# Moving attention's constants and the projections of sequence 0 into the LoRA stage before it, and the output bias from POOL to VectorE

## The chip, the cores and the metric

The kernel runs on one core of a Trainium2 chip. The metric is the device time in microseconds from launch to end; lower is better. Engines are named as in the profile: PE is TensorE (PEld its weight loads), DVE is VectorE, ACT is ScalarE, POOL is GpSimd and SP is SyncE, which issues the DMAs here.

## The reference

The program is a macaron block of six stages over 16 sequences of 512 tokens with 256 features. Each stage normalizes its input without learned scale and adds its result to `x`:

```
x = x + 0.5 * ffn(layernorm(x))       # 4-bit quantised feed-forward
x = x + mamba(layernorm(x))           # selective scan
x = x + 0.5 * ffn(layernorm(x))
x = x + 0.5 * lora(layernorm(x))      # base weights + 8 gated experts of rank 8
x = x + attention(layernorm(x))       # the stage that the change is about
x = x + 0.5 * lora(layernorm(x))
```

The two stages that matter compute, for one sequence:

```
lora:      result = x @ base_w.T + base_b
           gating = softmax(x @ router_w.T + router_b)      # in bf16
           mid    = x @ lora_A
           out    = result + 2 * einsum(mid, lora_B, gating)

attention: q, k, v = x @ Wq + bq, x @ Wk + bk, x @ Wv + bv  # 16 heads of 16
           scores  = q k^T / 4 + alibi, causal mask
           out     = softmax(scores) v  @ Wo + bo
```

## The kernel before

**Where the data lie.** From the third stage on, all 16 sequences stay in SBUF as tiles `x0` to `x15`, 128 partitions by 4 blocks of 128 tokens by 256 features, in float32. Attention and the LoRA stages read and write them in place.

**How the order comes about.** The kernel is written for a framework that gives each tile its place in memory, adds the waits between engines, and orders the instructions of each engine ahead of time by its own estimate of when they can run. An instruction can so be placed far ahead of where the text of the kernel has it, as far as free buffers allow. Attention's matmuls and transposes (`matmul`, `transpose`, lines 1175 to 1179) are kept in the order of the text; LoRA's are not. Tile pools that are opened one after the other share memory: a tile of a later pool waits for the last reader of the earlier tile in its place. In the kernel before, the pools of attention are opened when those of LoRA are closed.

**A LoRA stage** (`lora_phase`, lines 946 to 1060) runs as a pipeline over the sequences: in round `b`, `norm(b)` makes the normalized `xh`, `turn(b - 1)` transposes it into `xT`, `base(b - 2)` multiplies by base weights, router and `lora_A` at once (`ob`, line 998), adds to `x` and makes the softmax of the gates (lines 1002 to 1023), and `experts(b - 3)` transposes the gated rows (`ct`, line 1033), multiplies by `lora_B` (`o`, line 1042) and adds to `x` (line 1047). It runs twice, before attention and after it.

**Attention** (`attn_phase`) begins with constants: the four weights and five bias tiles by DMA (lines 1084 to 1098; `bob` is the output bias, spread over all partitions), row numbers, slopes, eight tiles each for `q` and `k` with the extra rows that carry ALiBi and the row maximum (lines 1132 and 1137), two masks, two tiles `mx` and three `va`. Then it projects sequence 0, all of it, ahead of its main loop.

`project(b)` is a generator that hands back control between pieces. The first piece is the LayerNorm on DVE (statistics, lines 1189 and 1190; `v`, line 1196; a logarithm and an exponential on ACT, lines 1198 and 1199, as a first guess of the inverse root; two Newton steps, lines 1201 to 1205; `xh`, line 1210) and, at its end, the output bias, added to `x` in advance by POOL (line 1214). Then come the transposes (line 1225 empties them), the products for q and k, whose rows SP copies head by head into the tiles of the ring (8 DMAs for each of 4 products, line 1249), and the values with their bias (`va`, line 1266).

The main loop goes over units of four heads, four units to a sequence, six steps to a unit. A step computes scores of unit `u` to find row maxima (`peak_score`; DVE adds the mask, line 1299, and takes the maximum, line 1303) and, interleaved, the scores of unit `u - 1` once more with the maximum subtracted (`weigh_score`), whose exponential ACT takes (`eT`, line 1349). Unit `u - 2` is multiplied with the values (`apply`), divided (`divide`) and, at the end of a sequence, multiplied by `Wo` and added to `x` (`close`, line 1407). Between the steps `aside` puts in pieces of the next sequence's `project` and of the last ones' `divide` and `close`, by costs written at each `yield`.

In the text of the kernel each product or transpose is one call; in the trace a float32 matmul or a transposed block shows as one or several records.

Of the kernel before, what the change touches and what calls it, by code (L numbers as in the profile page):

```python
# [8 lines left out]
F32 = mybir.dt.float32  # L9
# [26 lines left out]
def macaron_kernel(  # L36
# [909 lines left out]
    def lora_phase(weights, last):  # L946
        wx, lb, br = weights
        W = D + NE + NR
        with tc.tile_pool(name="l", bufs=2) as lp, tc.tile_pool(
# [101 lines left out]
            for b in range(NB + 3):  # L1051
                if 0 <= b - 3:
                    experts(b - 3)
                if 0 <= b - 2 < NB:
                    base(b - 2)
                if 0 <= b - 1 < NB:
                    turn(b - 1)
                if b < NB:
                    norm(b)
        return copies[-1]  # L1060


    def attn_phase(behind):
# [15 lines left out]
        with tc.tile_pool(name="aw", bufs=1) as aw, tc.tile_pool(  # L1079
            name="a", bufs=2  # L1080
        ) as ap, tc.tile_pool(name="a_s", bufs=1, space=PSUM) as ps_s, tc.tile_pool(
            name="a_ps", bufs=2, space=PSUM
        ) as ps:
            wp = {}
# [8 lines left out]

            bq_t = aw.tile([P, KD], F32, name="bq_t")
# [33 lines left out]
            qs, ks = [], []  # L1128
# [12 lines left out]
            qms = {}  # L1141

            def at(b, j):
                return (b % 2) * NJ + j
# [19 lines left out]
            mxs, vas = [], []  # L1164
            for r in range(3):
                if r < 2:
                    mx = aw.tile([P, NC4, 4, 32], F32, name=f"mx{r}")
                    nc.gpsimd.memset(mx, 0.0)
                    mxs.append(mx)
                va = aw.tile([P, NC4, VW], F32, name=f"va{r}")  # L1170
                nc.gpsimd.memset(va, 1.0)
                vas.append(va)


            def matmul(out, **kw):
                tc.keep_in_program_order(nc.tensor.matmul(out, **kw))  # L1176

            def transpose(out, in_):
                tc.keep_in_program_order(nc.tensor.transpose(out, in_, ident))  # L1179

            def project(b):

                x = xs[b]
                st = ap.tile([P, NC4, 6], F32, name="st", tag="st")
                mv = ap.tile([P, NC4, 2], F32, name="mv", tag="mv")
                for c in range(NC4):
                    nc.vector.bn_stats(out=st[:, c, :], in_=x[:, c, :])
                    nc.vector.bn_aggr(out=mv[:, c, :], in_=st[:, c, :])  # L1190


                v = ap.tile([P, NC4], F32, name="v", tag="v")
                g = ap.tile([P, NC4], F32, name="g", tag="g")
                rs = ap.tile([P, NC4], F32, name="rs", tag="rs")
                nc.vector.tensor_scalar(v, mv[:, :, 1], EPS, None, op0=ALU.add)  # L1196
                with tc.issue_after(loaded.ins):
                    nc.scalar.activation(rs, v, AF.Ln)
                nc.scalar.activation(rs, rs, AF.Exp, scale=-0.5)
                for _ in range(2):  # L1200
                    nc.vector.tensor_tensor(g, rs, v, op=ALU.mult)
                    nc.vector.scalar_tensor_tensor(
                        g, g, -0.5, rs, op0=ALU.mult, op1=ALU.mult
                    )
                    nc.vector.scalar_tensor_tensor(
                        rs, g, 1.5, rs, op0=ALU.add, op1=ALU.mult
                    )
                xh = ap.tile([P, NC4, D], F32, name="xh", tag="xh", bufs=1)
                for c in range(NC4):
                    nc.vector.tensor_scalar(  # L1210
                        xh[:, c, :], x[:, c, :], mv[:, c, 0:1], rs[:, c : c + 1],
                        op0=ALU.subtract, op1=ALU.mult,
                    )
                nc.gpsimd.tensor_tensor(  # L1214
                    xs[b], xs[b], bob.unsqueeze(1).to_broadcast([P, NC4, D]), op=ALU.add
                )
                yield 0, False
                xT = ap.tile([P, KD, SEQ], F32, name="xT", tag="xT", bufs=1)
                for k in range(KD):
                    p = ps.tile([P, SEQ], F32, name="p", tag="mm")  # L1220
                    for c in range(NC4):
                        transpose(
                            p[:, c * P : (c + 1) * P], xh[:, c, k * P : (k + 1) * P]
                        )
                    nc.scalar.copy(xT[:, k, :], p)
                    yield 2, False
                for m in range(KD):
                    for name, ring in (("q", qs), ("k", ks)):
                        p = ps.tile([P, SEQ], F32, name="p", tag="mm")
                        for k in range(KD):  # L1230
                            matmul(
                                p, lhsT=wp[name][:, k, m * P : (m + 1) * P],
                                rhs=xT[:, k, :], start=(k == 0), stop=(k == KD - 1),
                            )
                            if k == 0:
                                yield 3, True
                        r = ap.tile([P, SEQ], F32, name=f"{name}u", tag=f"{name}u")
                        if name == "q":
                            nc.scalar.activation(
                                r, p, AF.Identity, bias=bq_t[:, m : m + 1], scale=0.25  # L1240
                            )
                        else:
                            nc.vector.tensor_scalar(
                                r, p, bk_t[:, m : m + 1], None, op0=ALU.add
                            )

                        for h in range(8):
                            i, j = h % 4, 2 * m + h // 4
                            nc.sync.dma_start(
                                out=ring[at(b, j)][32 * i : 32 * i + HD, :],  # L1250
                                in_=r[HD * h : HD * (h + 1), :],
                            )
                        yield 3, False
                for half in range(2):
                    p = ps.tile([P, 2, D], F32, name="p", tag="mm")
                    for c in range(2):
                        t = 2 * half + c
                        for k in range(KD):
                            matmul(
                                p[:, c, :], lhsT=xT[:, k, t * P : (t + 1) * P],  # L1260
                                rhs=wp["v"][:, k, :], start=(k == 0), stop=(k == KD - 1),
                            )
                        if c == 0:
                            yield 3, True
                    dst = vas[b % 3][:, 2 * half : 2 * half + 2, : NH * HV]
                    nc.vector.tensor_tensor(
                        dst.rearrange("p c (h e) -> p c h e", e=HV)[:, :, :, :HD],
                        p.rearrange("p c (h e) -> p c h e", e=HD),
                        bvb.rearrange("p (h e) -> p h e", e=HD).unsqueeze(1).to_broadcast(
                            [P, 2, NH, HD]  # L1270
                        ),
                        op=ALU.add,
                    )
                    yield 3, False


            def peak_score(b, j, part, pair, s):

                q, k = qs[at(b, j)], ks[at(b, j)]
                for n, (t, off) in enumerate(PEAK[part]):  # L1280
                    ln = (t + 1) * P
                    for i in range(2):
                        r0 = 32 * (2 * pair + i)
                        matmul(
                            s[:, i, off : off + ln],
                            lhsT=q[r0 : r0 + 32, t * P : (t + 1) * P],
                            rhs=k[r0 : r0 + 32, :ln],
                            start=(n == 0), stop=(n == len(PEAK[part]) - 1),
                            skip_group_check=True,
                        )  # L1290
                        yield

            def peak_max(b, j, part, pair, s):
                mx = mxs[(b * NJ + j) % 2]
                t, off = PEAK[part][0]
                w = len(PEAK[part]) * P

                own = s[:, :, off + t * P : off + t * P + w]
# [86 lines left out]
            def close(b, os):  # L1385
# [9 lines left out]
                for half in range(2):  # L1395
                    r = ps.tile([P, 2, D], F32, name="r", tag="mm")
                    for c in range(2):
# [6 lines left out]
                        if c == 0:  # L1404
                            yield 3, True
# [198 lines left out]
```

## Time and profile before

| What | Value |
|---|---|
| Time, median of three runs | 4422.94 us (4412.12 to 4426.61) |
| Profiled execution, its own time | 4425.58 us |
| Span of the profiled execution, first to last instruction | 4423.8 us |
| Mean granted TensorE clock | 0.960 |
| Start of the first LoRA stage (first load of its weights) | 2992.45 us |
| End of its last matmul | 3132.0 us |
| First score of attention | 3161.84 us |
| Start of the second LoRA stage (its first memset) | 4280.81 us |

Times of single instructions and windows below are microseconds from the start of this span. An answer of the timeline has start, length, engine, line, operation, output and inputs, shapes and count; a bracket at its end has the engine's idle time before it and what ended that. A window has its bounds and length, the busy time of PE, PEld, DVE, ACT and POOL with the number of instructions in brackets, the granted clock of TensorE (1.00 is full), the share of the DMA engines and GB/s. A row of the waits reads: engine, tile and line, what it waited for, microseconds in all, times, the longest.

### The profile page before, as it was taken

What the parts mean: (1) busy time and instruction counts of PE and PEld (TensorE: products, weight loads), DVE (VectorE), ACT (ScalarE), POOL (GpSimd) and SP (SyncE); (2) the same over time, 40 slices, a digit from 0 to 9 for tenths busy, and PEclk for the clock granted to TensorE, in tenths of its full rate; (3) what the DMA queues carried; (4) which work ended last, traced back from release to release, by engine and by line L of the source; (5) the groups of instructions that cost most, each with busy time, mean ns of one, the idle gap of its engine ahead of it and who ended that gap; (6) DMA issues with size and microseconds to landing.
All of it is one profiled execution on the core that took longest, in us unless ns stands there. A gap on an engine that the chain in (4) does not pass through costs nothing. (4 is left out here: it accounts for less than half of the span.)

```text
span 4423.8 us, 51434 instructions
## 1 busy us (share of the span) xinstructions
PE 4037.3 (91%) x18786; PEld 2208.9 (50%) x18786; DVE 3744.2 (85%) x4919; ACT 2333.3 (53%) x3485; POOL 1680.5 (38%) x965
## 2 busy tenths in 40 slices
PE   7999978888888898988887999998899999999988
PEld 4666633333333333333333666766455555555546
DVE  9999839999999999999999899987677777777755
ACT  4444346777777777777664444436233334344345
POOL 3000038888888888888888000000100000000000
PEclk9999989999999999999999999999799999999979
DMA  4000033444444444444441200000100000000002
GB/s 147 15 20 15 15 132 126 135 136 137 132 137 136 135 139 137 126 135 133 133 137 39 103 1 1 1 1 4 32 11 18 18 16 18 15 18 18 13 8 69
DMA packets 120895, 305.16 MB, mean 69 GB/s; under 512 B 25329, under 2 KB 45362, under 8 KB 104002
## 3 DMA queue, kind: packets, MB, share of 16 engines
q1 hardware_dynamic: 120642, 301.88, 21.7%
q8 instruction: 148, 2.42, 0.2%
q14 instruction: 105, 0.86, 0.1%
HBM read 239.68 MB, written 45.35 MB: 64 GB/s over the span
## 5 line engine op out<-in xcount | busy, mean ns | idle before, releaser
L486 POOL TENSOR_TENSOR bx<-dtu,bc 128x1024 f32<-128x1024 f32 x512 | 1193.6, 2358 | 47.5 <-DVE h L882 47.4
L492 PE MATMUL y<-g,ident 128*128 128x512 f32 x2048 | 1007.3, 630 | 130.1 <-DVE g L489 129.8
L882 DVE TENSOR_TENSOR_SCAN h<-da,bx 128x1024 f32<-128x1024 f32 x384 | 879.7, 2291 | 85.5 <-ACT da L483 48.6
L483 ACT ACTIVATE da<-dt,a_neg 128x511 f32<-128x511 f32 x1024 | 702.9, 688 | 217.7 <-DVE hs L882 117.6
L492 PEld LDWEIGHTS y<-g,ident 128*128 128x128 f32 x2048 | 389.0, 199 | 709.3 <-issue 461.2
L1349 ACT ACTIVATE eT<-s 128x768 f32<-128x768 f32 (+1 forms) x384 | 338.2, 881 | 495.1 <-PE s L1176 495.1
L1176 PE MATMUL s<-k,q 32*128 32x256 f32 (+3 forms) x2048 | 500.3, 498 | 1.2 <-DMA k<-ku 1.2
L489 DVE TENSOR_TENSOR g<-h,bc 128x1024 f32<-128x1024 f32 x384 | 468.8, 1221 | 28.6 <-DVE h L882 1.4
L1176 PE MATMUL s<-qm,k 32*128 32x512 f32 (+3 forms) x2048 | 409.5, 497 | 37.3 <-ACT eT L1349 37.2
L1299 DVE TENSOR_TENSOR s<-s,mask 128x256 f32<-128x256 f32 (+1 forms) x384 | 199.8, 520 | 263.1 <-PE s L1176 256.8
L1303 DVE TENSOR_REDUCE mx<-s 128x2 f32<-128x1024 f32 (+3 forms) x512 | 409.7, 821 | 12.2
L1214 POOL TENSOR_TENSOR x<-x,bob 128x1024 f32<-128x1024 f32 x16 | 37.5, 2342 | 880.4 <-DVE xh L1210 878.0
L486 POOL TENSOR_TENSOR g<-hs,bc 128x1024 f32<-128x1024 f32 x128 | 301.2, 2353 | 157.7 <-DVE hs L882 140.5
L290 ACT ACTIVATE sl<-g 128x352 f32<-128x352 f32 x256 | 118.0, 464 | 385.2 <-PE g L285 380.4
L1176 PEld LDWEIGHTS s<-k,q 32*128 32x128 f32 x2048 | 232.1, 199 | 172.7 <-issue 95.3
L957 POOL MEMSET cb<- 128x4 f32 x6 | 0.3, 105 | 779.4 <-PE o L330 561.3
L882 DVE TENSOR_TENSOR_SCAN hs<-da,bx 128x1024 f32<-128x1024 f32 x128 | 292.0, 2281 | 2.5 <-ACT da L483 2.5
L492 PE MATMUL p<-xT,w_in 128*128 128x512 f32 x500 | 242.3, 608 | 19.7 <-ACT xT L483 10.0
L1176 PEld LDWEIGHTS s<-qm,k 32*128 32x128 f32 x2048 | 181.9, 198 | 86.0 <-ACT eT L1349 80.3
L483 ACT ACT_TABLE_LOAD x170 | 218.1, 1283 | 3.0
L515 POOL MEMSET xs<- 128x12 f32 x2 | 0.2, 110 | 513.9 <-DMA xd<-x 513.9
L285 PE MATMUL g<-wgT,xT 128*128 128x352 f32 x512 | 182.6, 467 | 0.0
(240 smaller groups left out, 6950.0 us busy)
## 6 DMA issues: line engine op xcount, KB each, us to landing
bc<-bd SPq DMA_DIRECT2D x128, 1024.0 KB, 6.5
xs<-xc SPq DMA_DIRECT2D x240, 256.0 KB, 4.7
xc<-xp SPq DMA_DIRECT2D x60, 256.0 KB, 2.0
x<-_attn_hidden_states_dram SPq DMA_DIRECT2D x16, 512.0 KB, 7.2
xd<-x SPq DMA_DIRECT2D x16, 512.0 KB, 2.6
xo<-xd SPq DMA_DIRECT2D x16, 512.0 KB, 3.5
xe<-xo SPq DMA_DIRECT2D x16, 512.0 KB, 2.6
x<-xe SPq DMA_DIRECT2D x16, 512.0 KB, 10.2
```

Of the source, the lines that this page charges most:

```text
L285: nc.tensor.matmul(dst, lhsT=xT[:, k, c * P : (c + 1) * P], rhs=w[:, k, f0 : f0 + HF], start=(k == 0), stop=(k == KD - 1),)
L290: nc.scalar.activation(sl, g, AF.Silu)
L483: return tc.keep_in_program_order(nc.scalar.activation(out, in_, func, **kw))
L486: tc.keep_in_program_order(nc.gpsimd.tensor_tensor(out, in0, in1, op=op))
L489: tc.keep_in_program_order(nc.vector.tensor_tensor(out, in0, in1, op=op))
L492: tc.keep_in_program_order(nc.tensor.matmul(out, **kw))
L882: tc.keep_in_program_order(nc.vector.tensor_tensor_scan(flat(h), flat(das[t % 2]), flat(bxs.pop(t)), 0.0, op0=ALU.mult, op1=ALU.add,))
L1176: tc.keep_in_program_order(nc.tensor.matmul(out, **kw))
L1214: nc.gpsimd.tensor_tensor(xs[b], xs[b], bob.unsqueeze(1).to_broadcast([P, NC4, D]), op=ALU.add)
L1299: nc.vector.tensor_tensor(own, own, mask[:, :w].unsqueeze(1).to_broadcast([P, 2, w]), op=ALU.add)
L1303: nc.vector.tensor_reduce(mx[:, t, 2 * pair : 2 * pair + 2, RM], s[:, :, off : off + (t + 1) * P], axis=AX.X, op=ALU.max,)
L1349: nc.scalar.activation(eT[:, 2 * pair : 2 * pair + 2, e0 : e0 + w], s[:, :, :w], AF.Exp)
```

## The change

The constants of attention become a generator, `constants`, with pauses; the first LoRA stage draws from it in rounds 1 to 15, one piece a round and two in odd rounds, the rest in round 15. Their pool `aw` is opened ahead of LoRA's pools. Sequence 0, whose LoRA result is complete after round 15, is normalized in round 16 by LoRA's own `norm` (square root and reciprocal), transposed in round 17 by LoRA's `turn`, and projected by `heads`, the second half of the old `project`, which now takes its transposed input, its pools and its matmul as arguments: the first q and k products in round 17, the others and the values in round 18. Attention's own pools are opened after that, where LoRA's were. The second LoRA stage has neither argument and is as before. For every sequence the POOL add of `bob` goes, and DVE adds it in two halves after the values. The rest of the diff is indentation and names.

```diff
-    def lora_phase(weights, last):
+    def lora_phase(weights, last, beside=None, heads=None):
 ...
                 if b < NB:
                     norm(b)
+                if heads is not None:
+                    if 0 < b < NB:
+                        next(beside, None)
+                        if b % 2:
+                            next(beside, None)
+                    if b == NB - 1:
+                        for _ in beside:
+                            pass
+                    if b == NB:
+                        norm(0)
+                    if b == NB + 1:
+                        turn(0)
+                        first = heads(0, xTs.pop(0), lp, ps, "tr", nc.tensor.matmul)
+                        for _ in range(4):
+                            next(first)
+                    if b == NB + 2:
+                        for _ in first:
+                            pass
 ...
-    def attn_phase(behind):
+    def attn_phase(weights):
 ...
+        def constants(aw):
             # weights, bvb, bob by DMA
+            yield
             # bq_t, bk_t, prow, is_s, neg_m, slope, pos
+            yield
             for i in range(2):
                 for j in range(NJ):
                     # one q and one k tile
+                    yield
             # id16, mask, mask_k
+            yield
             # mx, va
 ...
         def project(b):
 ...
-                nc.gpsimd.tensor_tensor(
-                    xs[b], xs[b], bob.unsqueeze(1).to_broadcast([P, NC4, D]), op=ALU.add
-                )
                 yield 0, False
                 # transposes into xT
+            yield from heads(b, xT, ap, ps, "mm", matmul)
+
+        def heads(b, xT, ap, ps, tag, matmul):
             # q and k products with their DMAs
             for half in range(2):
                 # values with bvb into va
+                xc = x[:, 2 * half : 2 * half + 2, :]
+                nc.vector.tensor_tensor(
+                    xc, xc, bob.unsqueeze(1).to_broadcast([P, 2, D]), op=ALU.add
+                )
                 yield 3, False
 ...
+        with tc.tile_pool(name="aw", bufs=1) as aw:
+            behind = lora_phase(weights, False, constants(aw), heads)
+            # attention's pools, table load after behind, main loop
-            for _ in project(0):
-                pass
 ...
-    behind = lora_phase(weights, False)
-    attn_phase(behind)
+    attn_phase(weights)
     lora_phase(weights, True)
```

## The prediction

> **What bounds the kernel now.** I read the page first, then the chain of waits and the waits at the seam between the first LoRA stage and attention, then the timeline of two attention sequences, then windows cut at what those showed.
>
> ```profile
> span 4423.8 us, 51434 instructions
> ...
> PE 4037.3 (91%) x18786; PEld 2208.9 (50%) x18786; DVE 3744.2 (85%) x4919; ACT 2333.3 (53%) x3485; POOL 1680.5 (38%) x965
> ...
> L1214 POOL TENSOR_TENSOR x<-x,bob 128x1024 f32<-128x1024 f32 x16 | 37.5, 2342 | 880.4 <-DVE xh L1210 878.0
> ```
>
> TensorE carries the time. POOL's bias add seems cheap: 37.5 us in all on an engine that is free in attention. What it costs others is not in that row. The waits around the seam:
>
> ```profile
> POOL prow L1101 <- PE o L1042: 139.5, 1, 139.5
> ...
> SPq L1087 <- PE o L1042: 136.7, 1, 136.7
> ```
>
> All of attention's constants wait for the last LoRA matmul. The windows of the seam (busy time of each engine, then granted clock, DMA share, GB/s):
>
> ```profile
> 3132.03:3145.22 13.19, 0.00 (x1) 0.04 (x1) 12.49 (x53) 0.00 (x0) 5.90 (x11) 0.50 0.33 100
> 3145.22:3161.84 16.62, 14.65 (x41) 7.63 (x41) 12.77 (x41) 3.03 (x8) 4.69 (x2) 0.84 0.09 20
> 3161.84:3191.13 29.29, 28.13 (x71) 10.74 (x70) 18.31 (x40) 3.08 (x6) 2.35 (x1) 0.60 0.20 44
> ```
>
> TensorE is idle for 13.19 us while VectorE makes constants, then projects sequence 0 for 16.62 us; the first score is at 3161.84. Third, the timeline at one POOL add, and at a later one (start, length, engine, line):
>
> ```profile
> 3929.34 2.34 POOL L1214 TENSOR_TENSOR x<-x,bob 128x1024 f32<-128x1024 f32 x1 [65.93 <-DVE xh L1210]
> 3929.71 2.00 DVE L1196 TENSOR_SCALAR v<-mv 128x4 f32<-128x4 f32 x1
> ...
> 3931.74 0.20 ACT L1198 ACTIVATE rs<-v 128x4 f32<-128x4 f32 x1 [3.48 <-DVE v L1196]
> ...
> 3932.09 0.79 ACT L1349 ACTIVATE eT<-s 128x768 f32<-128x768 f32 x1
> ...
> 3932.93 1.00 PE L1176 MATMUL s<-qm,k 32*128 32x384 f32 x1 [2.29 <-ACT eT L1349]
> ```
> ```profile
> 3997.41 0.81 ACT L1349 ACTIVATE eT<-s 128x768 f32<-128x768 f32 x1 [0.88 <-PE s L1176]
> ...
> 3997.61 2.35 POOL L1214 TENSOR_TENSOR x<-x,bob 128x1024 f32<-128x1024 f32 x1 [65.93 <-DVE xh L1210]
> ...
> 3998.27 0.58 PE L1176 MATMUL s<-qm,k 32*128 32x384 f32 x1
> ```
>
> A VectorE instruction of 4 elements takes 2.00 us beside the add; where it meets no POOL work the same line takes 0.17. ScalarE's logarithm waits for it, the exponential of the scores is queued behind that logarithm, and TensorE waits 2.29 us for the exponential. At 3997 no later sequence is left to normalize, so `v` isn't there, and nothing waits. The windows from add to add show the price:
>
> ```profile
> 3929.34:3932.20 2.86, 1.30 (x4) 0.29 (x2) 2.33 (x5) 0.43 (x3) 2.34 (x1) 1.00 0.00 0
> 3932.20:3939.02 6.82, 6.09 (x33) 3.72 (x34) 4.39 (x12) 2.19 (x4) 0.00 (x0) 0.50 0.16 34
> 3939.02:3997.61 58.59, 58.26 (x493) 31.54 (x492) 44.00 (x74) 24.54 (x32) 0.00 (x1) 1.00 0.07 16
> 3997.61:4060.34 62.73, 62.40 (x529) 34.02 (x528) 47.48 (x79) 26.78 (x35) 2.36 (x2) 1.00 0.08 18
> ```
>
> A sequence with the wait takes 68.27 us (the first three rows), one without it 62.73 with the same 529 matmuls. The wait also halves the clock for 6.82 us. Period less period, 5.54 us.
>
> **The change part by part.**
>
> *The seam.* From the last base matmul's end (3123.8) to the first score 38.0 us pass now. After the change TensorE has, from 3123.8: eight transposes of sequence 0 (1.04, from 3108.94), `ct` 0.60 and `o` 1.97 of the last sequence (from 3112 to 3121), four q and k tiles at 1.88 (the wk group at 3150.96 at full clock) 7.5, values 3.62: 14.7 us, so 3138.5, and some 1.5 for tiles that wait to be emptied: 3140. The other path is SP's queue, which the 32 q and k transfers keep whole: transposes 1.0, copy 0.6, q tile 1.9, activation 0.67, eight issues at 0.62, two of k at 0.62, landing 2.0: 3136.2. TensorE ends last. Gain 3161.84 - 3140 = 22 us. Bounds: 26 if the DMAs set it, 16 if LayerNorm of sequence 1, whose scratch now comes out of the memory that LoRA releases, holds up TensorE (its four bn_stats at 0.41, aggregates, two Newton steps and `xh` 1.37 make some 5 us with its scalar steps, of which the projections cover most).
>
> *Constants inside LoRA.* VectorE takes 11.1 us for them (3132.74 to 3143.87), and sequence 0 adds its statistics (2.4), two ku (1.5), two va (1.4). From 3000 to 3132 VectorE waits 16.2 us for `ob`, 12.8 for `o`, 6.6 for `ex`: 35.6 against 16.4, so they hide under TensorE's matmuls; uncovered they cost 16. The eight constant DMAs (0.47 us of SP each) pass an SP queue that is empty there. The scaling of bq waits in VectorE's queue for its DMA, with LoRA's evictions behind it and TensorE behind those: 0 to 4 us (bob landed in 4.0), I take 1. The extra square-root and exponential tables are 2 x 1.28 on ScalarE, which idles 3.5 us in each late LoRA iteration; 0, or 2.6 if uncovered. POOL's memsets, iotas and selects, 6.2 us, now run beside LoRA's VectorE work. Beside a memset, slope took 1.10 and the first two q 1.07 and 1.24 where others take 0.15 and 0.47: 2.3 us lost now; I take 1 of it on the path. [...]
>
> *The bias on VectorE.* Sixteen POOL adds of 2.34 go; 32 VectorE adds come, 128x512, nearest row x<-x,r at 0.68: 1.37 us a sequence, 22 in all. VectorE is busy 50.7 of 68.27 us and would be at 50.7 - 1.83 + 1.37 = 50.2 of some 64, with its idle time mostly waits for TensorE's scores. So the adds hide, from 0 to 22 us; I take 2, because the row of waits has VectorE waiting for scores, not the reverse. Queued behind an add are the mask and maximum of a score tile, and TensorE waits for them only when both score tiles are full.
>
> *The stall.* Without POOL, `v` takes 0.17 instead of 2.00 and everything behind it moves up 1.83: TensorE's idle falls from 2.29 to 0.46 and the matmul starts at 3931.10. In the clean period it starts 0.66 after the add's start, which is here 3930.00. So 1.10 of 5.54 us stays, provided the clock holds; 0.46 idle is nearer to the clean period, where the clock was 1.00, than to 2.29. Gain 4.44 a period. Eleven periods have the stall (67.01, nine of 68.27, one more of 68.27): 11 x 4.44 = 49. Bounds: 0 and 59.6 (749.67 less 11 x 62.73).
>
> [...]
>
> Sum: 22 + 49 - 2 (adds) - 1 (bq) - 1 (POOL in LoRA) = 67. The profiled execution took 4425.6 (span 4423.8 and 1.8 around it): 4358.6. It stands 2.6 over the median of the runs, so 4356.
>
> **The rivals.** *Only the seam.* The adds become ready as soon as `xh` is made, just where VectorE is full. If they stand before `v`, the exponential is again 1.37 late, the idle comes to 1.8, the clock drops as before, and the period gains 0.46: 22 - 4 + 11 x 0.46 = 23, so 4400. For it: VectorE is at 2.33 of 2.86 us there. Against: then a mask gets in before `v`, and the exponential isn't held.
>
> *All of it.* The LayerNorm step moves away from the exponential (+10), and the slow start, 0.60 from 3161.84 to 3191.13, keeps a full clock (up to 29.3 x 0.4 = 12): 4334; and up to 12 more if LoRA takes nothing and sequences 1 and 2, 0.85 in the window 3191.13 to 3247.94, run clean: 4322.
>
> *Slower.* Each sequence gets a new idle of TensorE behind one VectorE add (0.68) beside a stall that stays, and the clock, falling once more, loses 3.41: 16 x 4.1 = 66 against 22 - 4 from the seam: +48, 4471. It decides if TensorE's idle in one window passes a point that lies between 0.46 and 2.29 us, and does so twice a sequence. Against it: VectorE waits for scores most of the time.
>
> *It doesn't do what it says.* Constants or q/k transfers are placed so late that attention starts no earlier, and the adds take the stall's place: about 4420.
>
> **How the numbers follow.** Likeliest case 0.53, only the seam 0.23, all of it 0.12, none 0.05, slower 0.07. The range, 4322 to 4408, takes the first three with their bounds and leaves out the last two. A measurement tells 0.3% (13 us) from no change. Faster by more: 0.87 (the first three less one part in a hundred); same 0.06; slower 0.07.
>
> **What would show it.** Right: constants' lines lie before the last LoRA matmul, no TensorE gap over 3 us at the seam, the first score some 22 us earlier counted from the last base matmul; no instruction on `v` near 2 us; periods of 62.7 to 64.5 us at clock 1.00. Wrong: periods still of 68.27 with a half-clock piece; LoRA longer by over 5 us up to its last base matmul; VectorE's adds in the chain ahead of scores.

## The result and the profile after

The changed kernel takes 4380.25 us (median of four runs, 4372.74 to 4381.85) against 4424.77 for the kernel before on the same chip (four runs, 4412.12 to 4427.87): a ratio of 0.9901 [0.9879, 0.9924]. It is faster by 44 us, not by the 67 of the forecast; 4380 lies in the range, 24 us above 4356. The profiled execution took 4381.85 us. First the page of the changed kernel (span; busy time, share and instructions of each engine):

```profile
span 4380.1 us, 51398 instructions
...
PE 3998.6 (91%) x18786; PEld 2189.6 (50%) x18786; DVE 3730.8 (85%) x4942; ACT 2340.5 (53%) x3492; POOL 1643.4 (38%) x949
```

The same 18786 matmuls are busy for 38.7 us less: the clock is halved for less time (61 us between 3130 and 4100, against 133 before). POOL loses 16 instructions and 37 us, the bias adds.

**The seam.** The waits of the changed kernel from 3130 to 3200 (us in all, times, longest), and its windows from shortly after the last base matmul (3124.8):

```profile
PE p L1201 <- DVE xh L1233: 15.1, 1, 15.1
...
DVE st L1212 <- DMA k<-ku: 5.6, 1, 5.6
```
```profile
3125.00:3140.21 15.21, 13.72 (x52) 8.39 (x50) 6.17 (x14) 4.44 (x7) 0.00 (x0) 1.00 0.15 36
3140.21:3156.43 16.22, 1.14 (x8) 0.31 (x8) 9.20 (x37) 0.82 (x4) 0.00 (x0) 0.62 0.14 33
3156.43:3182.00 25.57, 25.57 (x62) 10.39 (x62) 19.37 (x60) 3.70 (x8) 0.00 (x0) 0.51 0.10 21
```

The waits for constants are gone, and the first score stands at 3140.21: 15.4 us after the last base matmul, where 38.0 passed before. That is the forecast's 22 to the first score. But in the second window TensorE works 1.14 of 16.22 us, and in the third it is full at clock 0.51. The 13.19 us of idle time before the first score has turned into 15.09 us behind it. The timeline of the changed kernel says why:

```profile
3140.21 1.14 PE L1198 MATMUL s<-k,q 32*128 32x512 f32 x8 [0.78 <-DVE va L1291]
...
3143.97 4.96 SPq L1274 DMA_DIRECT2D k<-ku  x8
...
3150.45 0.75 DVE L1212 BATCH_NORM_STATS2 st<-x 128x6 f32<-128x256 f32 x2 [5.59 <-DMA k<-ku]
...
3156.43 0.80 PE L1201 MATMUL p<-ident,xh 128*128 128x128 f32 x2 [15.09 <-DVE xh L1233]
```

The statistics of sequence 1 (L1212) wait for the last transfers of sequence 0's keys, data that they do not read. Their tile lies in attention's pool, which takes LoRA's memory, and there lie the `ku` tiles that these transfers read. The transposes of sequence 1 stand ahead of the next scores in TensorE's fixed order, so TensorE waits for that LayerNorm too. The next landmark is `qm`: there VectorE adds the first unit's row maxima to `q`, and no score can be weighed before it. The last base matmuls (`ob`) and the first `qm`, before and then after:

```profile
3122.71 1.08 PE L998 MATMUL ob<-lw_x,xT 128*128 128x272 f32 x4
...
3184.53 0.69 DVE L1318 TENSOR_TENSOR qm<-q,p 128x512 f32<-128x512 f32 x1 [0.58 <-PE p L1179]
```
```profile
3123.74 1.08 PE L1000 MATMUL ob<-lw_x,xT 128*128 128x272 f32 x4
...
3176.17 0.69 DVE L1348 TENSOR_TENSOR qm<-q,p 128x512 f32<-128x512 f32 x1 [0.60 <-PE p L1201]
```

The first `qm` comes 51.35 us after the end of the last base matmul, 60.74 before. 9.4 us are left of the 22.

**A sequence.** The changed kernel's timeline at one LayerNorm:

```profile
3889.80 1.29 DVE L1300 TENSOR_TENSOR x<-x,bob 128x512 f32<-128x512 f32 x2
...
3891.41 0.17 DVE L1219 TENSOR_SCALAR v<-mv 128x4 f32<-128x4 f32 x1
...
3891.62 0.20 ACT L1221 ACTIVATE rs<-v 128x4 f32<-128x4 f32 x1 [2.73 <-DVE v L1219]
...
3891.97 0.79 ACT L1379 ACTIVATE eT<-s 128x768 f32<-128x768 f32 x1
...
3892.81 0.59 PE L1198 MATMUL s<-qm,k 32*128 32x384 f32 x1 [1.54 <-ACT eT L1379]
```

`v` takes 0.17 us, not 2.00, as forecast. But two bias adds, 1.29 us, stand ahead of it in VectorE's queue: those of the sequence before, whose `xh` has just been made. The logarithm, the exponential behind it and TensorE are late by these: TensorE's idle time falls from 2.29 to 1.54, not to 0.46. The windows, one sequence late in the stage and one earlier drop of the clock:

```profile
3889.80:3954.64 64.84, 62.97 (x529) 34.16 (x529) 49.89 (x92) 27.00 (x37) 0.00 (x0) 1.00 0.08 18
```
```profile
3303.18:3304.72 1.54, 0.06 (x1) 0.00 (x0) 1.51 (x7) 1.11 (x4) 0.00 (x0) 0.95 0.00 0
3304.72:3311.50 6.78, 6.73 (x34) 3.72 (x34) 4.79 (x15) 2.15 (x3) 0.00 (x0) 0.51 0.17 36
```

Counted from the first `qm` of a sequence to that of the next, a period is 64.84 us at full clock from the fifth on. The first four are 71.21, 67.37, 66.32 and 65.30. In the second and third of them the clock drops (at 3304.57 and 3372.84) after gaps of the same 1.54 us that later cost no clock.

### The profile page after: what moved, and what is told of

Its sections match the earlier page's. It is cut to its first block, busy times and chain, and to the rows that moved or that the text cites. A ratio compares the mean times of both kernels' runs of the same rounds, so it can differ in the third digit from the quotient of the medians.

```text
span 4380.1 us, 51398 instructions
## 1 busy us (share of the span) xinstructions
PE 3998.6 (91%) x18786; PEld 2189.6 (50%) x18786; DVE 3730.8 (85%) x4942; ACT 2340.5 (53%) x3492; POOL 1643.4 (38%) x949
## 5 line engine op out<-in xcount | busy, mean ns | idle before, releaser
L1198 PE MATMUL s<-k,q 32*128 32x256 f32 (+3 forms) x2048 | 484.5, 483 | 0.8 <-DVE va L1291 0.8
L1198 PE MATMUL s<-qm,k 32*128 32x512 f32 (+3 forms) x2048 | 394.6, 481 | 29.3 <-ACT eT L1379 29.3
L1198 PEld LDWEIGHTS s<-k,q 32*128 32x128 f32 x2048 | 223.1, 190 | 161.6 <-issue 84.5
L285 PE MATMUL g<-wk,xT 128*128 128x352 f32 x512 | 182.6, 467 | 0.0
```

The costliest lines, as they stand in the source:

```text
L285: nc.tensor.matmul(dst, lhsT=xT[:, k, c * P : (c + 1) * P], rhs=w[:, k, f0 : f0 + HF], start=(k == 0), stop=(k == KD - 1),)
```

## The experiments

Landmarks below are from each run's own profiled execution; "to `qm`" counts from its last base matmul. From the first load of its weights up to that matmul the first LoRA stage takes 132.75 us with the constants (changed kernel) and 131.34 without (kernel before).

**Each half alone.** `e1_bias_only` is the kernel before with the adds on VectorE:

```diff
-                nc.gpsimd.tensor_tensor(
-                    xs[b], xs[b], bob.unsqueeze(1).to_broadcast([P, NC4, D]), op=ALU.add
-                )
 ...                                    # after the values of each half
+                    xc = x[:, 2 * half : 2 * half + 2, :]
+                    nc.vector.tensor_tensor(
+                        xc, xc, bob.unsqueeze(1).to_broadcast([P, 2, D]), op=ALU.add
+                    )
```

> The kernel before with only the bias moved to VectorE, two adds a sequence after the values; constants and sequence 0 stay behind LoRA. Theory (the POOL add held VectorE's v, v held ScalarE's queue, that held TensorE, and the idle halved the clock; the two parts of the change are independent): sequence periods as in the changed kernel, 64.8 us instead of 68.27, worth 35 us, and about 4 us more at the seam, where two VectorE instructions took 2.0 us beside POOL adds on the chain: 4386 us. Rival (the clock that the seam leaves behind decides whether the periods run clean): periods stay at 68.27 and the time at 4415 to 4425.

Measured: 4378.07 us (4373.67 to 4378.53), ratio 0.9896 [0.9881, 0.9911]. One half of the change is as fast as the whole. Its periods are 64.85 from the second sequence on, with the gap of 1.54, and none of these drops the clock.

`e2_seam_only` is the changed kernel with the adds on POOL again, at the end of each LayerNorm:

```diff
+        def add_bias(b):
+            nc.gpsimd.tensor_tensor(
+                xs[b], xs[b], const["bob"].unsqueeze(1).to_broadcast([P, NC4, D]), op=ALU.add
+            )
 ...                                    # project(b) and, for sequence 0, heads
+            add_bias(b)
 ...
-                xc = x[:, 2 * half : 2 * half + 2, :]
-                nc.vector.tensor_tensor(
-                    xc, xc, bob.unsqueeze(1).to_broadcast([P, 2, D]), op=ALU.add
-                )
```

> The changed kernel with the bias back on POOL, at the end of LayerNorm as before; constants and sequence 0 stay within LoRA. Theory: the seam alone is worth the 8 us by which the first row maxima came earlier (3184.5 to 3176.2), and the periods are 68.27 again with v near 2.0 us: 4417 us. Rival (the seam's clock cures the periods): 4380 to 4390.

Measured: 4408.54 us (4405.88 to 4417.24), ratio 0.9971 [0.9960, 0.9983]: 15 us faster by the medians, 17.7 in the profile. To `qm` it gains 8.2 us (52.54 against 60.74); the first period takes 71.4 instead of 75.5, and the next three take 66.2 to 66.6 instead of 68.27, with a half clock of 3.41 us or none instead of 6.83. From the fifth on the periods are 68.26 again. Its timeline and windows at 3369, where the same stall cost no clock, and at 3503, where it did:

```profile
3368.58 2.34 POOL L1204 TENSOR_TENSOR x<-x,bob 128x1024 f32<-128x1024 f32 x1 [64.78 <-DVE xh L1238]
3368.95 2.00 DVE L1224 TENSOR_SCALAR v<-mv 128x4 f32<-128x4 f32 x1
...
3372.17 0.58 PE L1198 MATMUL s<-qm,k 32*128 32x384 f32 x1 [2.29 <-ACT eT L1383]
```
```profile
3372.20:3379.00 6.80, 6.80 (x60) 3.87 (x64) 6.59 (x17) 2.93 (x4) 0.00 (x0) 1.00 0.18 40
...
3505.20:3512.00 6.80, 6.80 (x38) 3.67 (x38) 4.91 (x12) 1.83 (x3) 0.00 (x0) 0.58 0.18 39
```

After 2.29 us of idle time the clock is 1.00 in one place and 0.58 in another, in one kernel. The length of the gap alone does not decide.

The two halves do not add: from the last base matmul to the end `e1` gains 45.1 us, `e2` 17.7, the whole change 44.7.

**Where the seam's gain went.** `e3_own_pool` is the changed kernel with a pool for LayerNorm and projections that is opened before LoRA's, so that sequence 1 need not wait for LoRA's memory:

```diff
+    with tc.tile_pool(name="aw", bufs=1) as aw, tc.tile_pool(name="pj", bufs=2) as pj:
+        pools["proj"] = pj
 ...
-                        turn(0)
-                        first = heads(0, xTs.pop(0), lp, ps, "tr", nc.tensor.matmul)
+                        x0T = proj.tile([P, KD, SEQ], F32, name="xT", tag="xT", bufs=1)
+                        transpose_seq(xhs.pop(0), x0T, ps, "tr")
+                        first = heads(0, x0T, proj, ps, "tr", nc.tensor.matmul)
 ...
-            ap, ps = pools["sbuf"], pools["psum"]
+            ap, ps = pools["proj"], pools["psum"]
```

> The changed kernel with the tiles of LayerNorm and projection (st, mv, v, g, rs, xh, xT, qu, ku) in a pool that is opened before LoRA's pools and used for sequence 0 too, so that the LayerNorm of sequence 1 waits for nothing of LoRA's. Theory (LayerNorm of sequence 1 waits, by the shared memory, for the last k transfer of sequence 0, and TensorE waits 15.09 us for it at half a clock after): first score still near 3140, no gap over 3 us behind it, first row maxima some 15 us earlier, 4362 us (4355 to 4367). Rival (the scores of sequence 0 wait for the k transfers anyway, whatever the memory): the gap stays in another place, 4376 to 4382.

Measured: 4355.01 us (4352.57 to 4359.10), ratio 0.9848 [0.9834, 0.9861]: 25 us below the change's median. The windows of the same two places:

```profile
3140.43:3154.50 14.07, 11.68 (x57) 5.29 (x58) 13.90 (x35) 2.17 (x5) 0.00 (x0) 1.00 0.21 50
3154.50:3182.00 27.50, 27.22 (x204) 14.04 (x203) 22.81 (x43) 10.81 (x13) 0.00 (x0) 1.00 0.14 33
```

The idle 15 us are gone (TensorE is busy 11.68 of 14.07), and so is the half clock behind them. The first `qm`,

```profile
3154.52 0.68 DVE L1349 TENSOR_TENSOR qm<-q,p 128x512 f32<-128x512 f32 x1
```

stands 29.75 us after the last base matmul, 21.6 sooner than after the change. The wait was one for memory.

**The bias.** `e4_no_bias` is the changed kernel without the lines of the VectorE add; `bo` is left out of the result.

```diff
-                xc = x[:, 2 * half : 2 * half + 2, :]
-                nc.vector.tensor_tensor(
-                    xc, xc, bob.unsqueeze(1).to_broadcast([P, 2, D]), op=ALU.add
-                )
```

> The changed kernel without the output bias: bo is left out, nothing takes the adds' place. It prices the 32 VectorE adds. Theory (the two adds stand between xh and v and hold the exponential by 1.3 us each sequence, so TensorE still idles 1.54): period 64.84 becomes 63.5 to 63.8, 11 to 14 sequences, 4364 us. Rival (the adds hide in VectorE's waits, and the rest of the period is LayerNorm itself): period 64.8, 4379 us.

Measured: 4368.58 us (4367.46 to 4373.06), ratio 0.9880 [0.9866, 0.9893]. Its timeline and a whole period:

```profile
3812.30 0.17 DVE L1219 TENSOR_SCALAR v<-mv 128x4 f32<-128x4 f32 x1
...
3813.70 0.58 PE L1198 MATMUL s<-qm,k 32*128 32x384 f32 x1 [0.46 <-ACT eT L1375]
```
```profile
3749.86:3813.73 63.87, 63.07 (x532) 34.10 (x532) 49.14 (x94) 27.00 (x37) 0.00 (x0) 1.00 0.08 18
```

These are the prediction's 0.46 and 63.83, to 0.04 us. The adds on VectorE, charged there with 2 us in all, cost 64.84 - 63.87 = 0.97 a period. In the changed kernel they cost the early drops of the clock as well: `e4` has the same 15 us of idle time at the seam, but no period after the first has a drop, and its first eleven take 707.7 us against 723.6.

**Without moving the add.** `e5_ln_direct` leaves the kernel before and its POOL add as they are, and lets ScalarE take the logarithm from `mv` itself, so that nothing on the path to the exponential waits for `v`:

```diff
-                    nc.scalar.activation(rs, v, AF.Ln)
+                    nc.scalar.activation(rs, mv[:, :, 1], AF.Ln, bias=eps)
```

> The kernel before, POOL add and seam as they were; only ScalarE's logarithm reads the variance itself, with the epsilon as its bias, and no longer waits for VectorE's v. Theory (the wait reaches TensorE through ScalarE's queue): v still takes 2.0 us beside the POOL add, but the exponential is issued some 1.8 us earlier, TensorE's idle falls from 2.29 to some 0.5 us, the clock holds, period 63.9 to 64.9 instead of 68.27, 4376 to 4387 us. Rival (the 1.83 us that VectorE loses hold mask and maximum, and TensorE waits for its score tiles instead): period over 67, 4410 to 4424.

Measured: 4391.91 us (4385.08 to 4395.20), ratio 0.9938 [0.9925, 0.9952], between the two theories, with a period of 65.69. Its timeline:

```profile
3446.88 2.35 POOL L1214 TENSOR_TENSOR x<-x,bob 128x1024 f32<-128x1024 f32 x1 [63.34 <-DVE xh L1210]
3447.25 2.00 DVE L1196 TENSOR_SCALAR v<-mv 128x4 f32<-128x4 f32 x1
...
3448.54 0.58 PE L1176 MATMUL s<-qm,k 32*128 32x384 f32 x1 [0.36 <-ACT eT L1349]
...
3451.95 0.48 PE L1176 MATMUL s<-k,q 32*128 32x256 f32 x1 [1.36 <-DVE mx L1303]
```

The path through the logarithm is broken, as expected: 0.36 us there. But `v` still blocks VectorE for 2 us; what queues behind it, masks and maxima, is late, and TensorE pays 1.36 us three microseconds later. In `e8` below, with the same edit and a `v` of 0.17 us, TensorE has no such gap. So the stall had two ways to TensorE.

**A faster version.** `e6_close_vector` is `e3` with the two adds moved to `close`, right after the addition of the output product, where no LayerNorm is near:

```diff
-                xc = x[:, 2 * half : 2 * half + 2, :]      # in heads
-                nc.vector.tensor_tensor(
-                    xc, xc, bob.unsqueeze(1).to_broadcast([P, 2, D]), op=ALU.add
-                )
 ...
+                nc.vector.tensor_tensor(                   # in close, after x += r
+                    xc, xc, const["bob"].unsqueeze(1).to_broadcast([P, 2, D]), op=ALU.add
+                )
```

> The own-pool version with VectorE's two bias adds moved to the end of each sequence's attention, each after the add of its output product, so that they can't stand between xh and v. Theory (an add costs only by where it stands): period 63.9 as without bias, 4342 us. Rival (VectorE's 1.37 us a sequence cost wherever they stand): 64.8, 4355 us.

Measured: 4345.74 us (4342.98 to 4349.62), ratio 0.9836 [0.9822, 0.9849]. The adds' 0.98 a period is gone. By the medians it is 9 us below `e3`, but the kernel before was 4 us faster beside `e5` to `e8` (4419.6) than beside `e1` to `e4` (4423.5), and the two intervals overlap. In the profiles, from the last base matmul to the end, it is 8.6 us shorter (1219.4 against 1228.0). A period of it, and one of its last sequences, with no LayerNorm:

```profile
3731.16:3795.02 63.86, 63.06 (x532) 34.09 (x532) 50.24 (x96) 26.98 (x37) 0.00 (x0) 1.00 0.08 18
3997.60:4060.33 62.73, 62.40 (x533) 33.97 (x532) 47.37 (x76) 26.80 (x35) 0.00 (x0) 1.00 0.08 18
```

`e7_close_pool` puts the same adds, in the same place, on POOL:

```diff
-                nc.vector.tensor_tensor(
+                nc.gpsimd.tensor_tensor(
```

> The same with the adds at the end of each sequence on POOL. Theory (POOL holds VectorE only where VectorE works on SBUF alone: LayerNorm; mask and maximum read PSUM): no VectorE instruction near 2 us, period 63.9, 4341 us. Rival (a POOL add beside any VectorE work costs TensorE its score tiles, or meets LayerNorm again): period 65 to 68, 4355 to 4400.

Measured: 4345.69 us (4343.65 to 4348.02), ratio 0.9836 [0.9822, 0.9849], the same. Its timeline, POOL's row and then VectorE's from another answer:

```profile
3632.16 1.27 POOL L1437 TENSOR_TENSOR x<-x,bob 128x512 f32<-128x512 f32 x1 [10.03 <-DVE x L1436]
...
3632.15 0.70 DVE L1325 TENSOR_TENSOR s<-s,mask 128x512 f32<-128x512 f32 x1
3632.76 0.26 DVE L1405 RECIPROCAL ri<-p 128x16 f32<-128x16 f32 x1
```

Beside POOL's 1.27 us the mask add takes 0.70 and the reciprocal 0.26, against means of 0.70 and 0.25 in the kernel before: neither is held, and from the first score to the last no VectorE instruction takes over 1.23 us. That fits the expectation's reason, that mask and maximum read PSUM, and the kernel before, where beside POOL's adds `v` takes 2.00 us and one Newton step (at 3151.09) 2.11, masks and maxima 0.42 to 0.96; but not all work on SBUF alone is held either (the statistics beside POOL's memsets, below). So the engine that adds the bias does not matter; the place does.

`e8_ln_direct_e6` adds the edit of `e5` to `e6`:

```diff
-                nc.scalar.activation(rs, v, AF.Ln)
+                nc.scalar.activation(rs, mv[:, :, 1], AF.Ln, bias=eps)
```

> The version with VectorE's adds at the end of each sequence, and ScalarE's logarithm on the variance itself. Theory: what is left of the wait (0.46 us of TensorE, 1.1 us a period over the clean 62.7) is v and the two activations ahead of the exponential; one of the three goes: period 63.6, 4338 us. Rival (the rest is VectorE's LayerNorm work itself): 63.9, 4342 us.

Measured: 4343.32 us (4339.86 to 4349.91), ratio 0.9831 [0.9817, 0.9846]. The gap goes from 0.46 to 0.35, the period stays 63.86, as the rival had it; the difference to `e6` is within the runs' spread. Shortening this last gap no longer shortens a period. The 1.13 us over the 62.73 of the last sequences split in `e6`'s windows into 0.47 of idle time (0.80 against 0.33) and 0.66 of longer busy time; where the latter comes from stays open.

## Why the prediction was right and wrong

By span the forecast was 4423.8 - 67 = 4356.8; measured are 4380.1, 23.3 more. The time lies in the range because the range reached far enough to hold the rival *only the seam* (4400); neither of the two large terms came out at its size. The terms:

| Term | Forecast gain | Measured | Where |
|---|---|---|---|
| Seam | 22 | 9.4 | from the last base matmul to `qm` |
| Stall less adds | 49 - 2 = 47 | 35.6 | from `qm` to the second LoRA stage |
| Constants in LoRA | -2 | -1.0 | up to the last base matmul |
| Second LoRA stage | 0 | -0.2 | from its first memset to the end, 143.0 to 143.2 us |

*The seam: the sum was right to its landmark, and the landmark was the wrong one.* The first score, forecast for 3140, came at 3140.21. In part that is luck: from the last base matmul TensorE worked 13.9 us and idled 1.5, 15.4 in all against 16.2 in the sum, and LoRA's end was 1.0 later. The failing step is the bound of 16 for the LayerNorm of sequence 1. The prediction had seen that its scratch takes LoRA's memory, priced the LayerNorm's own work at some 5 us and took it as covered. What it left out is what the memory waits for: not LoRA's last matmul but the 32 transfers that still read `ku` and `qu` from there. SP issues them one after the other from 3128.73 to 3148.93, and the last ends at 3150.4. The LayerNorm itself then took from 3150.45 to 3156.43, 6.0 us. The term of 22 was above what came, 9.4, and so was its lower bound of 16. `e3`, with memory of its own, gave the time back, 21.6 us to `qm`. Part of "no TensorE gap over 3 us at the seam" was wrong, too: the gap moved behind the first score.

The loss goes on past `qm`. The idle 15 us bring a half clock of 37.5 us from 3144 on, and three more pieces up to 3376. From 3130 on that makes 61.4 us, in 49.0 of which TensorE works; in `e1`, whose idle time at the seam is 13.2, it is 48.3, and TensorE works in 35.1 of them. The whole change leads `e1` by 57.3 - 51.4 = 5.9 us at `qm` and gives back 6.4 over the next four sequences (270.2 against 263.8). So the seam is worth nothing on top of the bias add, and 15 us alone.

*The stall: mechanism and size right, a term beside it missized.* `e4` confirms the reasoning to 0.04 us a period. But the adds were taken as hidden, at 2 us of a bound of 22. They cost 11 x 0.98 = 10.8: a sequence's adds become ready when its `xh` is made, VectorE starts the next sequence's LayerNorm right behind that `xh`, and the adds stand in its queue between this `xh` and that LayerNorm's `v`. That is the mechanism of the rival *only the seam*, which had idle time of 1.8 and got 1.54; the argument against it, that a mask would get in and the exponential not be held, was wrong. The rival's other half, that the clock would go on dropping, was wrong: it held from the fifth sequence on. 48.8 - 10.8 leaves 38.0; the second to fourth period, with their two drops of the clock, take 4.5 more (67.37 + 66.32 + 65.30 less 3 x 64.84), which `e4` does not have; that is 33.5, where the first eleven periods gained 758.1 - 723.6 = 34.5.

*The cost within LoRA* was small, as forecast. By the table it is 1.0 us of the 2 charged, and by the stage's own length 1.4; but `e1` and `e5`, whose first LoRA stage has no constants either, take 130.5 for it, 2.2 less than the change. POOL's memsets and row numbers run from 2992 to 2997, beside statistics from SBUF to SBUF that keep their 0.4 us and a scaling of LoRA's weights (`lw_x`, 128x512) that takes 1.35 where it takes 0.41 in the kernel before. `v` takes 2.00 us beside a POOL add and 0.17 in every kernel without one there. What decides which VectorE instruction is stretched beside POOL is not shown.

*The clock.* The eleven periods gave 34.5 us, and a drop followed idle time of 1.54 us at 3303. That the clock would hold at 0.46 us of idle time, as the prediction took from its rows, came true (`e4`: 0.46, clock 1.00). But the rows were read too simply, as a point between 0.46 and 2.29 us of idle time: the same 2.29 dropped the clock at 3503 in `e2` and not at 3370, and 1.54 dropped it at 3303 in the changed kernel and not at 3892.

*The rival "slower"* needed a second gap a sequence behind the adds. The adds came into the gap that was there, and no gap was added.

## What to carry to other kernels

When work is moved ahead of a stage, follow the path to the second thing that the stage does, not to its first instruction: the memory that the moved work borrows is held until its transfers have read it, and whoever gets that memory next waits for them, here VectorE for 5.6 us and TensorE, behind it, for 15.1. When a small operation is moved to another engine, ask where in that engine's queue it becomes ready and what short link of a long chain stands behind it: here 1.3 us of adds in the wrong place cost 0.97 us of every period, and the same adds at the end of the sequence left the period at 63.86, as without them, on either engine.

## What the runs showed of the hardware

From the first LoRA stage on, the half-clock pieces of TensorE come in lengths that are multiples of 3.41 us (3.41, 6.83, 10.24, 13.65, 23.89, 37.55), but for the one at the very end, and whether a gap brings one depends on more than its length. The stretches below are 3.41 us long, their bounds counted in steps of that length from a change of the clock: the one that holds most of the 1.54 us at 3303 in the changed kernel, and then the two that share the 2.29 us at 3370 in `e2`:

```profile
3301.16:3304.57 3.41, 2.08 (x10) 0.67 (x6) 3.38 (x13) 0.96 (x3) 0.00 (x0) 1.00 0.00 0
```
```profile
3367.58:3370.99 3.41, 2.31 (x14) 0.67 (x6) 3.34 (x9) 0.01 (x1) 2.34 (x1) 1.00 0.02 5
3370.99:3374.40 3.41, 2.23 (x18) 1.30 (x22) 3.31 (x13) 2.49 (x5) 0.00 (x0) 1.00 0.05 12
```

In the first TensorE idles 1.33 us, and the clock drops at its end. In the other two it idles 1.10 and 1.18, and the clock holds. The idle time of such a stretch does not decide alone either: in the kernel before, the clock falls at 3215.40 after one with 0.28 us of it. Both steady periods of the two kernels are multiples of the length: 68.27 is 20.0 times 3.41 us, and the clock drops in each (before); 64.84 is 19.0 times, and it drops in none (after, from the fifth period on). 63.86 and 65.69 are no multiples and dropped no clock either.

What decides is not shown: no run varied the place of a gap alone.
